# First attention: row maxima through VectorE's transpose and transfers, and a visit for two groups of heads

## The chip, the cores and the metric

The kernel runs on one core of one Trainium2 chip. The metric is device time in microseconds (us) of one execution, the median of several runs. A core has TensorE (matrix products; it writes only to PSUM, eight banks here), VectorE, ScalarE, GpSimd (POOL in the profile) and SyncE (SP), which here only issues transfers. Each engine works through its own instructions in the order of the program and waits on semaphores.

## The reference, cut to what matters

Input `x` is 16 batches of 256 tokens of 128 channels. Four layers follow, each added to `x`: an attention with binarised weights (the one that is changed), a mixture of eight experts, a second attention with relative positions, the experts again. The first attention:

```python
def _binarize(W):
    alpha = jnp.mean(jnp.abs(W), axis=tuple(range(1, W.ndim)), keepdims=True)
    B = W + jax.lax.stop_gradient(jnp.sign(W) - W)
    return alpha * B
...
B, T, C = x.shape                      # 16, 256, 128
H = HEADS                              # 16
Dh = C // H                            # 8
scale = Dh ** (-0.5)
q = split_heads(_binlinear(x, Wq, bq))
k = split_heads(_binlinear(x, Wk, bk))
v = split_heads(_binlinear(x, Wv, bv))
att = jnp.einsum('bhtd,bhsd->bhts', q, k) * scale
att = jax.nn.softmax(att, axis=-1)
y = jnp.einsum('bhts,bhsd->bhtd', att, v)
y = y.transpose(0, 2, 1, 3).reshape(B, T, C)
return _binlinear(y, Wp, bp)
```

Its `x` is layer-normalised first. The experts need the gate's logits of all tokens, so the first attention's last steps for a batch also normalise the result, turn it to channels and compute the logits.

## The kernel before

**Groups.** A batch has 16 heads, handled as four groups (`NG`) of four heads (`NJ`). G counts groups over all batches, 0 to 63; batch b has groups 4b to 4b+3. The queries and keys of a batch lie in one tile `spread[b % 4]` (`a_qk` in the profile): head j of a group sits on partitions 32j to 32j+31, of which row 32j is a spare row and the next eight hold the head's eight channels. In the spare row the queries have 0 and the keys 1 (`aux`).

**Steps of a group.**

- `scores(G, j)` computes head j's 256 x 256 scores into one PSUM bank with two matmuls that use only the 32 rows of that head, so matmuls of different j can run beside one another. VectorE then reduces the bank to minus the row maximum (L458, `a_nm<-a_s`, a tile of two columns per head).
- `maxima(G)` turns those maxima with two full TensorE transposes against the identity (L467) and VectorE adds them to the queries (L473): the sum, `qaug` (`a_qa`), has minus the maximum of each query in its spare row.
- `exponentials(G, j)` multiplies keys by `qaug` (L481, `a_t`), so the scores arrive transposed and with the maximum taken off, since the spare row of the keys is 1. ScalarE takes the exponential (L487, `a_pT<-a_t`).
- `values(G)` handles two groups at once with 32 matmul passes of 32 columns each (L497); ScalarE copies the result (L506).

**Steps of a batch.** `channels` (transpose the normalised tokens, L406), `project` (queries and keys; ScalarE adds the bias, SP stores the result to DRAM at L423 and loads it back spread over the rows at L427, four loads), `project_v` (L436), `tokens` (transposes back and division by the sums, L514 to L524), `turn_back` (L532), `project_out` (L545, VectorE adds to `x`), `gate_channels` (L558) and `gate` (L566, logits).

**Order.** All engines follow the order in which the program was written. `together` runs generators in turns: first the TensorE part of each, then what reads it. The main loop runs over i, from 3 to 72. For each i it does two halves, each with `scores(i, ...)` of two heads and `exponentials(i-3, ...)` of the two *other* heads, and then `visit(i)`, which does the steps of batches that are due by `table` together with `maxima(i-1)` and, every second time, `values(i-4)`. So groups and visits alternate, and the exponentials follow the scores three groups later. `begin` sets up the first groups; in the last visits pieces of the following experts (`filling`) are put between.

**Banks.** `bank8` hands out the eight PSUM banks in a ring, and the loop reorders the ring after each group. A bank is written again only when its last reader is done.

**Weights.** `load_later` loads the second attention's weights and w1 after visit 5 and w2 after visit 9, each of w1 and w2 (2,048 KB) in one transfer.

Of the kernel before, what the change touches and what calls it, by code (L numbers as in the profile page):

```python
# [10 lines left out]
F32 = mybir.dt.float32  # L11
# [7 lines left out]
P = 128  # L19
# [27 lines left out]
def _consts():  # L47

    p = np.arange(P)
    parts = {  # L50
        "ident": np.eye(P),

        "aux": np.repeat(p[:, None] % 32 == 0, NG, axis=1),

        "mask_h": p[:, None] % DH == np.arange(DH)[None, :],
        "mask_q": p[:, None] // DH % DH == np.arange(DH)[None, :],

        "digits": np.tile(
            np.concatenate([np.arange(1.0, NCAND + 1) * (1 << z) for z in SHIFTS]), (P, 1)
        ),  # L60
    }
    at = 0
    for name, a in parts.items():
        CONSTS[name] = (at, at + a.shape[1])
        at += a.shape[1]
    return np.concatenate([a.astype(np.float32) for a in parts.values()], axis=1)
# [12 lines left out]
def hybrid_kernel(ctx: ExitStack, tc: tile.TileContext, io):  # L79
# [31 lines left out]

    def load_later(step):

        for name, t in ((("b_w", b_w), ("w1", w1)), (("w2", w2),))[step]:
            nc.sync.dma_start(t, io[name])
        if step:
            nc.vector.tensor_copy(flips, const("digits"))
# [80 lines left out]
    def attention_a(place, filling):  # L198
# [4 lines left out]
        with ExitStack() as st:  # L203
# [5 lines left out]
            ring = deque(range(8))  # L209

            def bank8(name):
                i = ring.popleft()
                ring.append(i)
                return psum.tile([P, 2, T], F32, tag=f"x{i}", name=name, bufs=1)
# [5 lines left out]
            def spread_tile(fill):  # L220
                i = len(spread)
                t = wpool.tile([P, 2, NG, T], F32, tag=f"qk{i}", name=f"a_qk{i}")
                if fill:
                    nc.gpsimd.memset(t[:, 0], 0.0)
                    nc.gpsimd.tensor_copy(
                        t[:, 1], const("aux").unsqueeze(2).to_broadcast([P, NG, T])
                    )
                spread.append(t)
# [23 lines left out]
            def fills():  # L252

                wS["w"] = pool.tile([P, T], F32, tag="sw", name="wS_w", bufs=1)
                nc.gpsimd.memset(wS["w"], 0.0)
                for n in "qk":
                    wS[n] = pool.tile([P, NG, NJ, 32], F32, tag="sgn", name=f"wS_{n}")
                    nc.gpsimd.memset(wS[n], 0.0)
                for i in range(4):
                    nm = wpool.tile([P, 2, NJ, 32], F32, tag=f"nm{i}", name=f"a_nm{i}")  # L260
                    nc.gpsimd.memset(nm, 0.0)
                    nms.append(nm)
                values_tile()
# [33 lines left out]
            def begin():  # L297
# [30 lines left out]
                for i, n in enumerate("qk"):  # L328
                    nc.vector.tensor_scalar(
                        wS[n][:, :, :, 1 : 1 + DH],  # L330
                        pt[:, i].rearrange("p (g j d) -> p g j d", g=NG, j=NJ),
                        SCALE if n == "q" else 1.0, None, ALU.mult,
                    )
# [29 lines left out]
                for i in range(2):  # L363
                    spread_tile(True)
                    values_tile()
                    if not i:
                        nc.gpsimd.memset(ones, 1.0)
                        together(*(scores(0, j) for j in range(NJ)))
                        second = matmuls(1)
# [3 lines left out]
                        together(maxima(0, bank8("a_mx0")[:, 0]))  # L373
                        together(project(1))
                        together(*second)

                ring.rotate(4)
                third = matmuls(2)
                turns = maxima(1, bank8("a_mx1")[:, 0])
                next(turns)  # L380
                next(third[0], None)
                next(turns, None)
                pt = bank8("a_mv2")
                together(project_v(0, pt[:, 0]), channels(2, pt[:, 1]))
                together(*third[1:])
                used = list(ring)
                ring.clear()
                ring.extend(used[:2] + used[6:] + used[2:6])
                xns[3] = normalise(3)
                spread_tile(True)  # L390

            def matmuls(G):

                parts = [scores(G, j) for j in range(NJ)]
                for _ in range(2):
                    for g in parts:
                        next(g)
                return parts

            q, k, va, xnT, qaug, probs, heads, ys, yTs = ({} for _ in range(9))  # L400
# [10 lines left out]
            def project(b):  # L411

                pp = bank8(f"a_pqk{b}")
# [11 lines left out]
                for j in range(NJ):  # L425
                    at = 32 * j + 1
# [3 lines left out]
                    )  # L430
                q[b], k[b] = to[:, 0], to[:, 1]
# [15 lines left out]
            def scores(G, j):  # L447
# [4 lines left out]
                for t in range(2):  # L452
                    nc.tensor.matmul(  # L453
                        sc[:, t, :], q[b][rows, g, t * P : (t + 1) * P], k[b][rows, g, :],
                        start=True, stop=True,
                    )
                    yield
                nc.vector.tensor_reduce(  # L458
                    nms[G % 4][:, :, j, 0:1].rearrange("p t o -> p (t o)"),
                    sc, AX.X, ALU.max, negate=True,  # L460
                )

            def maxima(G, pm):

                b, g = divmod(G, NG)
                for t in range(2):
                    nc.tensor.transpose(  # L467
                        pm[:, t * P : (t + 1) * P],
                        nms[G % 4][:, t].rearrange("p j e -> p (j e)"), ident,
                    )  # L470
                yield
                qaug[G] = work.tile([P, T], F32, tag="qa", name=f"a_qa{G}")
                nc.vector.tensor_tensor(qaug[G], q[b][:, g, :], pm, ALU.add)  # L473

            def exponentials(G, j):
# [4 lines left out]
                for t in range(2):  # L480
                    nc.tensor.matmul(  # L481
                        sc[:, t, :], k[b][rows, g, t * P : (t + 1) * P], qaug[G][rows, :],
# [25 lines left out]
            def tokens(b):  # L508

                ys[b] = work.tile([P, 2, C], F32, tag="y", name=f"a_y{b}")  # L510
                po = bank8(f"a_oq{b}").rearrange("p t (c x) -> p t c x", x=P)
# [50 lines left out]
            def gate(b, pl):  # L562
                pl = pl[:, 0 : 2 * NE].rearrange("p (t e) -> p t e", e=NE)
                for t in range(2):
                    at = b % 2 * T + t * P
                    nc.tensor.matmul(  # L566
                        pl[:, t, :], xn2[b // 2][:, at : at + P], gw, start=True, stop=True
                    )
# [10 lines left out]
            def of(b):  # L579
# [3 lines left out]
            n, own = NB * NG, []  # L583
# [10 lines left out]

            table = (
                ([], [(gate, -3)], [(turn_back, -2)]),
                ([(project, 2)], [(project_out, -2)], []),
                ([], [], [(channels, 3)]),
                ([(tokens, -1)], [], [(project_v, 2), (gate_channels, -2)]),
            )  # L600

            extra = {3: ([(project, 2)], [], [(project_v, 1)]), 4: ([], [], [(channels, 3)])}

            def visit(i):
                b, s = divmod(i, NG)
                alone, with_maxima, with_values = (
                    [(f, b + d) for f, d in pieces if of(b + d)] + more
                    for pieces, more in zip(table[s], extra.get(i, ([], [], [])))
                )
                parts = []  # L610
                if i < n + 1 or with_maxima:
                    pt = bank8(f"a_mx{i}")
                    if i < n + 1:
                        parts.append(maxima(i - 1, pt[:, 0]))
                    parts += [f(b, pt[:, 1]) for f, b in with_maxima]
                parts += [f(b) for f, b in alone]
                pair = s % 2 == 0 and i < n + 4
                if pair or with_values:
                    pt = bank8(f"a_mv{i}")
                    parts += [f(b, pt[:, k]) for k, (f, b) in enumerate(with_values)]  # L620
                    if pair:
                        parts.append(values(i - 4, pt[:, 1]))
# [3 lines left out]
            own_at = {2: 2, 3: 3, 4: 3, 5: 3, 6: 3, 7: 4, 8: 2}  # L626
            for i in range(3, NG * (NB + 2) + 1):
                b, s = divmod(i, NG)
                for half in range(2 if i < n else 0):
                    together(  # L630
                        *(scores(i, 2 * half + j) for j in range(2)),
                        *(exponentials(i - 3, 2 - 2 * half + j) for j in range(2)),
                    )
                if n <= i < n + 3:
                    together(*(exponentials(i - 3, j) for j in range(NJ)))
                if i < n:


                    used = list(ring)
                    ring.clear()  # L640
                    ring.extend(used[k] for k in (2, 0, 3, 1, 6, 4, 7, 5))
                if i >= n + 2:
# [3 lines left out]
                    for _ in range(own_at.get(i - n, 0)):  # L646
                        own.append(next(filling))
                visit(i)
                if i in (5, 9):
                    load_later(i // 9)  # L650
                if i == 4 or s == 2 and of(b + 4):

                    xns[b + 3 + (s == 2)] = normalise(b + 3 + (s == 2))
# [900 lines left out]
def _spread(v, extra):  # L1554

    out = np.zeros((NJ, 32, NG), np.float32)
    out[:, 0] = extra
    out[:, 1 : 1 + DH] = v.reshape(NG, NJ, DH).transpose(1, 2, 0)
# [72 lines left out]
```

## Time and profile before

| | us |
|---|---|
| median of 3 runs | 1523.93 (1523.55 to 1524.88) |
| the profiled execution | 1522.07 |
| its span, first to last instruction | 1520.0 |
| scores of the first attention, first to last start | 13.7 to 275.6 |
| exponentials' matmuls, first to last start | 21.9 to 284.0 |
| last logits of the first attention | 313.9 |

In rows of groups, the profile gives line, engine, operation, output<-input by the program's names and the count; then busy time in us and the mean of one in ns; then the idle time of the engine before them and what ended it. In timelines: start and length in us, engine, line, operation and count. In a row of a stretch: the stretch, then busy time of TensorE, its weight loads, VectorE, ScalarE and POOL, each with the number of instructions, then TensorE's granted clock (1.00 is full), the share of the transfer engines that was busy, and GB/s. An f32 matmul is recorded as two passes, a transpose as one. In waits: who waited for what, us in total, times, and the longest.

Sizes of the parts in question over the whole run:

| line | what | count | mean ns |
|---|---|---|---|
| L453, TensorE | scores, passes | 1024 | 389 |
| L481, TensorE | exponentials' matmuls, passes | 1024 | 392 |
| L467, TensorE | transposes of the maxima | 128 | 301 |
| L458, VectorE | row maxima | 256 | 682 |
| L473, VectorE | maxima added to the queries | 64 | 408 |
| L487, ScalarE | exponentials | 256 | 602 |
| L427, SP | loads of queries and keys | 60 | 297 to issue |

The mean of a pass includes filling and draining the array; passes that follow one another overlap.

### The profile page before, as it was taken

The numbers are of one execution on the slowest core, as the hardware profiler recorded it, in microseconds if no ns is written. First come the engines' busy times: TensorE is split into PE (matmuls) and PEld (weight loads), VectorE is DVE, ScalarE is ACT, GpSimd is POOL, SyncE is SP. The second block draws the span as 40 slices with busy tenths as digits, with TensorE's granted clock in tenths as the row PEclk, the third lists the DMA queues.
The fourth block names the chain that finished last, engine by engine and source line by source line (L and its number), as shares of the span: only waits on it lengthen the run. The fifth ranks groups of instructions, "written<-read, shape, count | busy, mean of one in ns | idle before, by whom it ended". The sixth has DMA issues, their size and how long they took to land. (4 is left out here: it accounts for less than half of the span.)

```text
span 1520.0 us, 35594 instructions
## 1 busy us (share of the span) xinstructions
PE 1500.0 (99%) x14318; PEld 878.5 (58%) x14318; DVE 1119.3 (74%) x2055; ACT 853.2 (56%) x2119; POOL 416.6 (27%) x521
## 2 busy tenths in 40 slices
PE   8999999999999999999899999999999999999998
PEld 6777777544444444445577777777544444455554
DVE  7887877335467788899799999999345458878843
ACT  4666666644434444444688888888644444444442
POOL 6333331100001000041388888897100000000000
PEclk9999999999999999999999999999999999999999
DMA  4511110000331202212122222222000440121220
GB/s 105 152 32 30 37 36 16 1 8 1 95 105 42 51 15 65 51 35 51 31 58 55 51 46 53 57 52 45 9 0 0 124 108 24 51 61 33 65 64 14
DMA packets 176732, 73.33 MB, mean 48 GB/s; under 512 B 75056, under 2 KB 175032, under 8 KB 176312
## 3 DMA queue, kind: packets, MB, share of 16 engines
q1 hardware_dynamic: 175928, 70.64, 19.7%
q8 instruction: 113, 1.85, 0.5%
q10 hardware_dynamic: 640, 0.42, 0.2%
q14 instruction: 51, 0.42, 0.1%
HBM read 51.04 MB, written 12.58 MB: 42 GB/s over the span
## 5 line engine op out<-in xcount | busy, mean ns | idle before, releaser
L1326 ACT ACTIVATE hT<-ph,head 128x512 f32<-128x512 f32 x320 | 220.1, 688 | 266.6 <-PE ph L1322 251.8
L1322 PE MATMUL ph<-xn,w 128*64 128x512 f32 (+1 forms) x1216 | 292.0, 593 | 0.5 <-ACT b_xnT L723 0.5
L901 ACT ACTIVATE b_pr<-b_s,b_nm 128x256 f32<-128x256 f32 x512 | 235.9, 473 | 62.4 <-DVE b_nm L896 62.0
L1340 DVE TENSOR_TENSOR hT<-hT,gb 128x1024 f32<-128x1024 f32 x144 | 178.4, 1239 | 38.3 <-ACT hT L1326 37.9
L1117 PE MATMUL py<-hT,w 128*128 128x512 f32 (+1 forms) x456 | 205.5, 594 | 1.0 <-ACT logits L987 0.5
L458 DVE TENSOR_REDUCE a_nm<-a_s 128x2 f32<-128x512 f32 x256 | 158.6, 682 | 50.5 <-PE a_t L481 49.3
L1322 PEld LDWEIGHTS ph<-xn,w 128*64 128x64 f32 (+1 forms) x1216 | 100.7, 140 | 146.5 <-issue 117.0
L1106 PE MATMUL ph<-xn,w 128*128 128x512 f32 x384 | 174.1, 594 | 2.4 <-ACT hT L1108 2.3
L1108 ACT ACTIVATE hT<-ph,head 128x512 f32<-128x512 f32 x192 | 131.0, 687 | 76.5 <-PE ph L1106 74.0
L896 DVE TENSOR_REDUCE b_nm<-b_s 128x4 f32<-128x1024 f32 x128 | 152.8, 1194 | 19.9 <-PE b_s L886 19.7
L886 PE MATMUL b_s<-b_kT,b_qd 64*64 64x256 f32 x1024 | 159.9, 382 | 3.5 <-ACT b_pr L901 3.5
L1377 PE MATMUL s_m<-mx,mix 128*64 128x256 f32 x576 | 158.6, 379 | 0.5 <-DVE mx L1346 0.5
L911 DVE STREAM_TRANSPOSE b_pT<-b_pr 128x1024 f32<-128x1024 f32 x128 | 157.2, 1228 | 0.0
L886 PE MATMUL b_s<-strip,b_qb 64*64 64x256 f32 x2048 | 156.6, 376 | 0.0
L886 PE MATMUL b_s<-b_kS,b_qd 64*64 64x256 f32 x1024 | 156.5, 382 | 0.0
L487 ACT ACTIVATE a_pT<-a_t 128x512 f32<-128x512 f32 x256 | 132.6, 602 | 29.6 <-PE a_t L481 29.3
L1377 PE MATMUL s_y<-hT,w 128*64 128x256 f32 x576 | 148.1, 379 | 0.0
L156 POOL TENSOR_SCALAR ve<-mv 128x2 f32<-128x2 f32 x64 | 16.3, 255 | 458.8 <-DVE mv L153 448.8
L1117 PEld LDWEIGHTS py<-hT,w 128*128 128x128 f32 x456 | 84.7, 191 | 94.6 <-issue 91.1
L481 PE MATMUL a_t<-a_qa,a_qk 32*128 32x256 f32 x1024 | 133.8, 392 | 0.1
L453 PE MATMUL a_s<-a_qk 32*128 32x256 f32 x1024 | 128.8, 389 | 0.3 <-ACT a_qkc L419 0.3
L1106 PEld LDWEIGHTS ph<-xn,w 128*128 128x128 f32 x384 | 72.0, 190 | 92.5 <-issue 83.8
(211 smaller groups left out, 2653.1 us busy)
## 6 DMA issues: line engine op xcount, KB each, us to landing
gb<-gd SPq DMA_DIRECT2D x128, 256.0 KB
w<-in_w SPq DMA_DIRECT2D x2, 2048.0 KB
a_qks<-a_qkc SPq DMA_DIRECT2D x15, 256.0 KB
a_qk<-a_qks SPq DMA_DIRECT2D x60, 64.0 KB
so<-sum SPq DMA_DIRECT2D x18, 128.0 KB
x<-in_x SPq DMA_DIRECT2D x16, 128.0 KB
b_qs<-b_qT SPq DMA_DIRECT2D x64, 32.0 KB
b_qsel<-b_qT SPq DMA_DIRECT2D x64, 32.0 KB
```

Source lines behind the costliest of these rows:

```text
L458: nc.vector.tensor_reduce(nms[G % 4][:, :, j, 0:1].rearrange("p t o -> p (t o)"), sc, AX.X, ALU.max, negate=True,)
L481: nc.tensor.matmul(sc[:, t, :], k[b][rows, g, t * P : (t + 1) * P], qaug[G][rows, :], start=True, stop=True,)
L886: nc.tensor.matmul(sc[64 * c : 64 * c + 64, r, u, :], (qb_[rows, at, c] if rel else qd[rows, at, x]).rearrange("p h q -> p (h q)"), strip[ ...
L896: nc.vector.tensor_reduce(nm, sc, AX.X, ALU.max, negate=True)
L901: nc.scalar.activation(pr[:, u, r, :], sc[:, r, u, :], AF.Exp, bias=nm[:, r, u : u + 1], scale=1.0, accum_out=sums[b][:, n : n + 1],)
L911: nc.vector.transpose(pT[:, half % 2, 4 * i : 4 * i + 4].rearrange("p n k h q -> p (n k h q)"), probs.pop(U).rearrange("p u r k -> p (u r ...
L1106: nc.tensor.matmul(ph, w1[:, m * P : (m + 1) * P], xn2[c], start=True, stop=True)
L1117: nc.tensor.matmul(py[:, 0:width], w2[:, e * NHC + k, :], hs[k], start=k == 0, stop=k == NHC - 1)
L1322: nc.tensor.matmul(ph[z], w1[:, m * P + z.start : m * P + z.stop], xn2[c], start=True, stop=True,)
L1326: nc.scalar.activation(h[:, k % 2], ph, AF.Gelu_apprx_tanh, bias=b1[:, m : m + 1], scale=1.0)
L1340: nc.vector.tensor_tensor(h, h, gb.unsqueeze(1).to_broadcast([P, 2, CH]), ALU.mult)
L1377: nc.tensor.matmul(acc[halves[z], col], a[:, k], b[:, k], start=e == 0 and region[i] not in region[:i], stop=e == NE - 1 and region[i] not ...
```

## The change

- **The spare row** moves from row 32j to row 32j+8, behind the eight channels. The keys' half of the tile is filled with 1 everywhere before the channels are loaded, so its spare row is 1; `aux` goes.
- **Row maxima.** `maxima` and `qaug` go. After the last head's reduction of a group, VectorE transposes the maxima in blocks of 32 x 32 (`turned`), and four transfers on SP, one per head, write them straight into the spare row of the queries. For that, the scores use every second token as stationary operand (`t::2`), so that a block holds 64 neighbouring tokens. `exponentials` reads the queries themselves.
- **Reset.** The scores need 0 in the spare row. From the fifth batch on, `project` adds a transfer that copies a row of zeros into it.
- **Order.** The loop runs over n; for each n the groups 2n and 2n+1 follow one another, each as two halves: `scores` of heads 0 and 1, then `exponentials` of heads 0 and 1 of the group four earlier, then the same with heads 2 and 3. After the two groups comes one `visit(n)` with the steps of two former visits, full-array steps ahead of those that use 32 columns, and `values` in every visit.
- **Gate.** The gate's two matmuls per batch become eight that use 32 columns each.
- **Banks** are handed out least recently used first.
- **Weights** are loaded in 17 transfers of 256 KB, one per visit from n = 3 on.

```diff
+    pieces = [(b_w, io["b_w"])]
+    for t, name in ((w1, "w1"), (w2, "w2")):
...
+        pieces += [(t[:, at : at + CH], flat[:, at : at + CH]) for at in range(0, NE * HID, CH)]
...
-            ring = deque(range(8))
-
-            def bank8(name):
-                i = ring.popleft()
-                ring.append(i)
+            used = [*range(8)]
+
+            def bank8(name, among=range(8)):
+                i = next(i for i in used if i in among)
+                used.remove(i)
+                used.append(i)
                 return psum.tile([P, 2, T], F32, tag=f"x{i}", name=name, bufs=1)
...
-                    nc.gpsimd.tensor_copy(
-                        t[:, 1], const("aux").unsqueeze(2).to_broadcast([P, NG, T])
-                    )
+                    nc.gpsimd.memset(t[:, 1], 1.0)
...
                 for j in range(NJ):
-                    at = 32 * j + 1
+                    at = 32 * j
...
+                if b >= 4:
+                    nc.sync.dma_start(to[DH::32, 0], to[DH + 1 :: 32, 0])
...
                     nc.tensor.matmul(
-                        sc[:, t, :], q[b][rows, g, t * P : (t + 1) * P], k[b][rows, g, :],
-                        start=True, stop=True,
+                        sc[:, t, :], q[b][rows, g, t::2], k[b][rows, g, :], start=True, stop=True
                     )
                     yield
+                nm = nms[G % 4]
                 nc.vector.tensor_reduce(
-                    nms[G % 4][:, :, j, 0:1].rearrange("p t o -> p (t o)"),
-                    sc, AX.X, ALU.max, negate=True,
-                )
-
-            def maxima(G, pm):
...
+                    nm[:, :, j], sc, AX.X, ALU.max, negate=True
+                )
+                if j < NJ - 1:
+                    return
+                turned = work.tile([P, 32, 2], F32, tag="nmT", name=f"a_nmT{G}", bufs=4)
+                nc.vector.transpose(turned.rearrange("p x t -> p t x"), nm)
+                for n in range(NJ):
+                    row = spread[b % 4][32 * n + DH : 32 * n + DH + 1, 0, g, :]
+                    nc.sync.dma_start(row, turned[n::32])
...
-                        sc[:, t, :], k[b][rows, g, t * P : (t + 1) * P], qaug[G][rows, :],
+                        sc[:, t, :], k[b][rows, g, t * P : (t + 1) * P], q[b][rows, g, :],
...
                 for t in range(2):
-                    at = b % 2 * T + t * P
-                    nc.tensor.matmul(
-                        pl[:, t, :], xn2[b // 2][:, at : at + P], gw, start=True, stop=True
-                    )
+                    for y in range(4):
+                        at = b % 2 * T + t * P + 32 * y
+                        nc.tensor.matmul(
+                            pl[32 * y : 32 * y + 32, t, :], xn2[b // 2][:, at : at + 32], gw,
+                            start=True, stop=True,
+                        )
...
+            shared = (
+                (
+                    [(tokens, -2)],
+                    [(channels, 2), (project_out, -3)],
+                    [(gate, -4)],
+                ),
+                (
+                    [(project, 2)],
+                    [(turn_back, -2), (gate_channels, -3)],
+                    [(project_v, 1)],
+                ),
+            )
...
+                    if valued:
+                        parts.append(values(pair, pt[:, 1]))
                 together(*parts)
...
-            for i in range(3, NG * (NB + 2) + 1):
-                b, s = divmod(i, NG)
-                for half in range(2 if i < n else 0):
-                    together(
-                        *(scores(i, 2 * half + j) for j in range(2)),
-                        *(exponentials(i - 3, 2 - 2 * half + j) for j in range(2)),
-                    )
...
+            own_at = {33: 2, 34: 3, 35: 3, 36: 3, 37: 4, 38: 5}
+            for n in range(1, 2 * NB + 7):
+                for i in (2 * n, 2 * n + 1):
+                    for half in range(2):
+                        if i < NG * NB:
+                            together(*(scores(i, 2 * half + j) for j in range(2)))
+                        if 0 <= i - 4 < NG * NB:
+                            together(*(exponentials(i - 4, 2 * half + j) for j in range(2)))
...
+                visit(n)
+                load_later(n - 3)
```

## The prediction, as put on record before the changed kernel was seen

> **What bounds the kernel now.** I read the page first, then the busy times of one steady stretch, then TensorE's own timeline, and last the two engines that empty its banks.
>
> ```profile
> PE 1500.0 (99%) x14318; PEld 878.5 (58%) x14318; DVE 1119.3 (74%) x2055; ACT 853.2 (56%) x2119; POOL 416.6 (27%) x521
> ...
> 151.03:167.86 16.83, 16.82 (x230) 12.36 (x227) 13.54 (x33) 11.14 (x25) 5.77 (x9) 1.00 0.15 34
> ```
>
> The second line is one batch of the first attention (four groups): 16.83 us, TensorE busy throughout at full clock (1.00), VectorE 13.54 of it, ScalarE 11.14. The three batches from 117.36 on all take 16.83 or 16.84. So TensorE's order sets the pace, and its timeline is the view to cost from:
>
> ```profile
> 151.03 0.44 PE L467 MATMUL a_mx<-head,a_nm 128*128 128x128 f32 x2
> 151.30 0.61 PE L545 MATMUL a_mx<-wp,a_yT 128*128 128x128 f32 x4
> 151.75 0.60 PE L415 MATMUL a_pqk<-a_xnT,wq 128*128 128x256 f32 x2
> 152.18 0.59 PE L415 MATMUL a_pqk<-a_xnT,wk 128*128 128x256 f32 x2
> 152.71 0.48 PE L453 MATMUL a_s<-a_qk 32*128 32x256 f32 x2
> 152.72 0.48 PE L481 MATMUL a_t<-a_qa,a_qk 32*128 32x256 f32 x2
> 153.03 0.38 PE L453 MATMUL a_s<-a_qk 32*128 32x256 f32 x2
> ...
> 153.47 0.58 PE L481 MATMUL a_t<-a_qa,a_qk 32*128 32x256 f32 x3
> 153.69 0.38 PE L453 MATMUL a_s<-a_qk 32*128 32x256 f32 x2
> ...
> 154.76 0.44 PE L467 MATMUL a_mx<-head,a_nm 128*128 128x128 f32 x2
> 155.04 0.38 PE L406 MATMUL a_mv<-head,xn 128*128 128x128 f32 x2
> 155.35 1.94 PE L497 MATMUL a_mv<-a_pT,a_va 128*32 128x256 f32 x32
> 157.22 0.48 PE L453 MATMUL a_s<-a_qk 32*128 32x256 f32 x2
> ```
>
> A record here is one pass; an f32 matmul of 256 columns has two. I subtract starts, since lengths overlap. Between 153.03 and 153.69 a step takes 0.22 us and holds four passes, two a_s and two a_t, one on each group of 32 rows. A group of heads is eight steps, 1.73 us; entering the 32-row shape costs 0.10 more (152.71 to 153.03 is 0.32) and leaving it 0.09. So 1.92 is the floor; the four groups of this batch take 2.05, 1.94, 2.17 and 1.98, together 8.15. The other 8.68 is visits: full-array passes of 0.112 (four in 151.30 to 151.75), or 0.215 with 256 columns, 0.15 for changing over, and 1.87 for values (155.35 to 157.22).
>
> **The change part by part.**
>
> *Removed from TensorE:* two transposes a group, 0.27 us (151.03 to 151.30), 1.1 a batch, and two of four visits, each with its 0.15. The VectorE addition behind them goes too (64 of 408 ns); VectorE is not the bound over a batch, so I cost that at nothing.
>
> *The new visits,* by those units. Even: 10 full passes (tokens 4, channels 2, project_out 4) 1.12 + 0.15, the gate as 16 narrow passes four abreast, values 1.87. The gate's nearest row is the weight load of a 32-column tile:
>
> ```profile
> L497 PEld LDWEIGHTS a_mv<-a_pT,a_va 128*32 128x32 f32 x1024 | 30.7, 109 | 22.0 <-issue 4.9 <-ACT a_pT L487 0.8 <-DVE a_nm L458 0.3
> ```
>
> Four steps of 0.11 are 0.44; 0.4 (the same passes now) to 0.9 (steps of 0.22) bound it. Even sum 3.58. Odd: project 4 x 0.215 = 0.86, eight passes 0.90, 0.15, values 1.87: 3.78. Together 7.36, against 8.68: 1.32 saved a batch.
>
> *The two groups without a visit between.* Undisturbed they would take 16 x 0.216 + 0.19 = 3.64. But a group uses eight banks, all there are: s0 s1 e0 e1 s2 s3 e2 e3 (s scores, e exponentials, the digit the row group). Banks are taken least recently first, so each tile of the second group waits until the same tile of the first is read. And where scores of rows 0, 1 were paired with exponentials of rows 2, 3, now both lie on the same rows, so no exponential finishes before four matmuls of its row group. The readers:
>
> ```profile
> 153.95 2.07 ACT L487 ACTIVATE a_pT<-a_t 128x512 f32<-128x512 f32 x4 [0.30 <-PE a_t L481]
> ...
> 154.00 2.45 DVE L458 TENSOR_REDUCE a_nm<-a_s 128x2 f32<-128x512 f32 x4
> ```
>
> Four exponentials take 2.07 and one about 0.60: they start 0.49 apart. Four reductions take 2.45 and one 0.68: 0.59 apart. ScalarE starts 0.25 after the last pass has streamed (pass from 153.48, plus 0.22, to 153.95). In-order waits are seen here:
>
> ```profile
> 22.66 0.18 PEld L481 LDWEIGHTS a_t<-a_qa,a_qk 32*128 32x128 f32 x1 [0.50 <-ACT a_xnT L409]
> 22.67 0.19 PEld L453 LDWEIGHTS a_s<-a_qk 32*128 32x128 f32 x2
> ```
>
> The a_t load waits for ScalarE, whose copy ends 22.61 (0.05 to come back); the a_s loads of other row groups, free since 22.4, start only behind it. Now from the start of a stretch: s0 to s3 are full at 0.10 + 4 x 0.216 = 0.97, e0 to e3 at 1.83. Reductions start at 1.22 and end at 1.90, 2.49, 3.08, 3.67; exponentials start at 2.08 and end at 2.68, 3.17, 3.66, 4.15. The second group, with 0.05 back and 0.10 for a load not made ahead: s0 from 1.95, s1 from 2.54, e0 behind s0 from 2.91, e1 from 3.51. s2 stands in program order behind e1's wait (3.22) and runs to 4.18; s3 waits for the fourth reduction, 3.72, and runs 0.96 to 4.68; e3, its bank back at 4.20, follows to 5.54. Leaving 0.09: **5.63 for two groups**.
>
> From below: were e3 bound by its own bank alone, 4.20 + 0.86 + 0.09 = 5.15. From above: no row shows a row group with eight passes queued while another one starts, only a short lead (the third a_t of 153.47 starts at 153.68, ahead of the a_s at 153.69 that precedes it in the program). With no lead only neighbouring halves overlap, three steps of two passes (0.43) a half: 13 x 0.43 + 0.19 = 5.8. I take 5.65: the two mechanisms agree within 0.2.
>
> The Trainium skill, "TensorE: Matmul & The Clock Gate", Part 3, says matmuls are strictly first in, first out, across tiles too. The rows at 153.68 and 153.69 speak against it; by the page the stretch would be 5.8 and the total some 5 us above mine.
>
> *VectorE's transpose* of 128x64 has no row of its shape. The nearest, 128x1024 at 1,228 ns, gives 0.08 by size; the shortest VectorE copy (logits, 166 ns) is the likelier floor. I take 0.17, one a group, behind the fourth reduction, where the next wait is not VectorE's; 0 to 1.2 bounds it, and at 1.2 the second group's reductions end 1 us later, still ahead of the next stretch.
>
> *The transfers.* SP issues 256 more, and from the fifth batch on a reset per batch. An issue of such a load takes 297 ns:
>
> ```profile
> SPq L427 <- DMA a_qks<-a_qkc: 29.6, 15, 3.2
> ...
> 22.30 1.36 SPq L427 DMA_DIRECT2D a_qk<-a_qks  x4
> ```
>
> A group's four need 4 x 0.3 = 1.2. The worst they stand behind is project's turn on SP: 3.2 for its store to land, 1.36 for four loads, 0.3 for the reset, 0.43 for a weight piece, some 2 before it for ScalarE's turn: 7.3. With landing (3.2 again) 11.7. A row is turned about 3.8 into its stretch and read two stretches later, 15 us on: hidden, costing nothing. Were that cover gone, every wait for it would stand on TensorE. The reset is read three visits later, likewise hidden. Weights in 17 pieces replace three loads at visits that end long before their first use (after 284 us): nothing. POOL's fill is 0.95 instead of 1.06 us, three times, before the loop: nothing. Queries taken every second column as weights: loads are 185 ns under a 216 ns step; no row shows a stride, so 0 to a doubling (a score pass of 0.37), and I take 0.
>
> *Sum.* A batch: 2 x 5.65 + 7.36 = 18.66 against 16.83: +1.83. Sixty of 64 groups run scores and exponentials together: 15 batches, **+27.4**. At the edges one group's exponentials and one values (2.9) move behind the last scores, while first and last visits lack pieces in both kernels: -4 to +5, taken as 0. The profiled run took 1522.07 (span 1520.0), so 1549.5; the median shown, 1523.93, lies 1.86 above: **1551**.
>
> **The rivals.**
>
> *Banks come back in time.* Then a stretch is 3.64, a batch 14.64, 2.19 x 15 = 33 saved: 1491. For it: all the removed passes are real, and VectorE (13.5 less 1.6 of 14.64) and ScalarE (11.14) would fit on average. Against it: eight reductions at 0.59 need 4.7 us in a stretch of 3.64, and only eight banks hold them. The sign turns at a stretch of 4.74 (16.83 - 7.36, halved); the last exponential's bank alone gives 5.15. 9 in 100; a draw 2.
>
> *Strict order:* 5.8 a stretch, 15 x 2 x 0.15 more: 1556. For it, no deep lead is shown; against it, the short one is. 25 in 100.
>
> *Row transfers or dependencies reach TensorE.* If scores of a group waited for the previous group's rows in the same tile, 64 x about 3 us: 1740. Against: scores begin at 13.70 while ScalarE writes other groups' slices of that tile up to 14.65. A milder form, strided loads at the doubled price, adds 0.15 to eight steps per group at most: 64 x 1.2 = 77. 9 in 100 together.
>
> **How the numbers follow.** Forecast 55 in 100, the rivals 9, 2, 25, 9. Forecast and strict order reach from a stretch of 5.15 (30 x 0.5 = 15 less, and the edge's -4: 1532) to one of 5.8 with slow gates (15 x 0.46 = 7), waits of 0.3 a stretch that I do not see (9) and an edge of +3: 5 + 7 + 9 + 3, 1575. Faster means below 1520.9, slower above 1527.0: 0.2%, what a measurement of this kernel can tell. Faster 0.09, same 0.02, slower 0.89.
>
> **What would show it.** Right: from 60 us on, a stretch of a_s and a_t 5.5 to 5.8 long with gaps in which row groups stand, waits of a_s and a_t for a_nm and a_pT; visits of 3.6 and 3.8; no TensorE wait for a transfer. Wrong: stretches under 4.7, or TensorE waiting for a_qk transfers, or score passes more than 0.22 apart where nothing waits.

## The result and the profile after

| | median, us | runs | profiled execution | its span |
|---|---|---|---|---|
| before | 1523.88 | 1523.55 to 1524.88 (4) | 1522.07 | 1520.0 |
| after | 1546.49 | 1545.48 to 1548.74 (4) | 1545.72 | 1543.6 |

The changed kernel is slower: 1.0149 times the kernel before, interval 1.0132 to 1.0167, or 22.6 us. Forecast were 1551 within 1532 to 1575.

The lines of after that answer to the first two shown of before are the page's busy times and one batch in the view of windows. In the second the columns are length, busy time and number of instructions for PE, PEld, DVE, ACT and POOL, granted clock, DMA share and GB/s:

```profile
PE 1521.8 (99%) x14382; PEld 913.4 (59%) x14382; DVE 1113.8 (72%) x2055; ACT 855.1 (55%) x2119; POOL 416.3 (27%) x521
...
125.69:144.01 18.32, 18.32 (x234) 14.69 (x230) 13.25 (x32) 11.35 (x24) 5.76 (x10) 1.00 0.31 60
```

A batch has grown from 16.83 us to 18.32 or 18.33, in both batches I laid a window over. 15 batches at 1.49 or 1.50 more make 22.4, and the interval of the measured 22.6 us is 20.1 to 25.4, so the loss lies in the steady loop. The two traces agree: the last logits of the first attention come at 337.2 us instead of 313.9, 23.3 of the 23.6 us by which the spans differ. TensorE counts as busy throughout in both kernels at full clock. What changed is how much each microsecond does, and busy time doesn't show that; the timeline does. One stretch of two groups in after, TensorE (start, length, operation, passes):

```profile
125.69 1.14 PE L434 MATMUL a_s<-a_qk 32*128 32x256 f32 x8
126.66 0.38 PE L456 MATMUL a_t<-a_qk 32*128 32x256 f32 x2
126.67 0.49 PE L434 MATMUL a_s<-a_qk 32*128 32x256 f32 x2
126.88 0.38 PE L456 MATMUL a_t<-a_qk 32*128 32x256 f32 x2
...
128.20 0.49 PE L434 MATMUL a_s<-a_qk 32*128 32x256 f32 x2
...
129.40 0.48 PE L434 MATMUL a_s<-a_qk 32*128 32x256 f32 x1
...
130.16 1.24 PE L456 MATMUL a_t<-a_qk 32*128 32x256 f32 x8
131.32 0.48 PE L394 MATMUL a_m<-a_xnT,wq 128*128 128x256 f32 x1
```

and VectorE under it:

```profile
126.86 2.49 DVE L439 TENSOR_REDUCE a_nm<-a_s 128x2 f32<-128x512 f32 x4 [0.86 <-PE a_s L434]
129.38 0.25 DVE L445 STREAM_TRANSPOSE a_nmT<-a_nm 128x64 f32<-128x64 f32 x1
129.54 2.45 DVE L439 TENSOR_REDUCE a_nm<-a_s 128x2 f32<-128x512 f32 x4
```

From 125.69 to 131.32 is 5.64 us, against 3.64 for the same passes without a wait. For the first 0.97 us the eight passes are a_s alone, two row groups at work and two idle; then four row groups; then less and less. The four reductions of the first group run from 126.86 to 129.34, and the last tile of the second group's scores starts at 129.40, as the fourth bank comes back. When the next visit starts at 131.32, VectorE is at the last reduction of the second group (to 131.99). How much of the loss is VectorE's pace and how much the order on TensorE, the experiments part.

The whole batch, with the visits taken from the same timelines by subtracting starts:

| us | before | after, forecast | after, measured |
|---|---|---|---|
| four groups | 8.15 | 2 x 5.65 = 11.30 | 2 x 5.64 = 11.28 |
| even visit | | 3.58 | 3.24 |
| odd visit | | 3.78 | 3.81 |
| all visits | 8.68 | 7.36 | 7.05 |
| batch | 16.83 | 18.66 | 18.33 |

### The profile page after: what moved, and what is told of

Same layout as the page of the kernel before. It is cut to its first block, busy times and chain, and to the rows that moved or that the text cites. A ratio compares the mean times of both kernels' runs of the same rounds, so it can differ in the third digit from the quotient of the medians.

```text
span 1543.6 us, 36649 instructions
## 1 busy us (share of the span) xinstructions
PE 1521.8 (99%) x14382; PEld 913.4 (59%) x14382; DVE 1113.8 (72%) x2055; ACT 855.1 (55%) x2119; POOL 416.3 (27%) x521
## 5 line engine op out<-in xcount | busy, mean ns | idle before, releaser
L881 DVE STREAM_TRANSPOSE b_pT<-b_pr 128x1024 f32<-128x1024 f32 x128 | 157.2, 1228 | 0.0
L434 PE MATMUL a_s<-a_qk 32*128 32x256 f32 x1024 | 151.6, 410 | 0.0
L456 PE MATMUL a_t<-a_qk 32*128 32x256 f32 x1024 | 144.6, 375 | 0.0
```

The source lines that it names most:

```text
L434: nc.tensor.matmul(sc[:, t, :], q[b][rows, g, t::2], k[b][rows, g, :], start=True, stop=True)
L881: nc.vector.transpose(pT[:, half % 2, 4 * i : 4 * i + 4].rearrange("p n k h q -> p (n k h q)"), probs.pop(U).rearrange("p u r k -> p (u r ...
```

## The experiments

All times below are from runs beside the kernel before on the same chip (its median there is 1522.97 to 1523.57). "Stretch" and "group" are from the start of the first a_s pass to the start of the next visit.

**e1_rows: the same visits, the two halves of a group on different rows.** In after, scores and exponentials of one half lie on the same 32-row groups. Here they alternate on opposite ones, as before.

```diff
-                        if i < NG * NB:
-                            together(*(scores(i, 2 * half + j) for j in range(2)))
-                        if 0 <= i - 4 < NG * NB:
-                            together(*(exponentials(i - 4, 2 * half + j) for j in range(2)))
+                        together(
+                            *(scores(i, 2 * half + j) for j in range(2) if i < NG * NB),
+                            *(
+                                exponentials(i - 4, 2 - 2 * half + j)
+                                for j in range(2)
+                                if 0 <= i - 4 < NG * NB
+                            ),
+                        )
```

> Exponentials lie on the other two row groups again and are interleaved with the scores. Theory (same-row order delays the exponentials and the first group's reads of the banks): all four row groups run from the start, the second group's last tiles start behind the fourth reduction at 3.7 us and end one tile later, a stretch of 4.8 instead of 5.64: 30 x 0.85 = 25 us less, 1521. Rival (two groups without a visit are what costs, whatever the rows): 5.6 a stretch, 1546. Rival (strided weights, transfers): no change, 1546.

Measured: 1527.27 us, ratio 1.0029 (1.0019 to 1.004). The stretch is 4.97, the batch 2 x 4.97 + 7.05 = 16.99. Its TensorE timeline:

```profile
194.65 0.49 PE L434 MATMUL a_s<-a_qk 32*128 32x256 f32 x2
194.66 0.48 PE L456 MATMUL a_t<-a_qk 32*128 32x256 f32 x2
...
196.28 1.37 PE L434 MATMUL a_s<-a_qk 32*128 32x256 f32 x4
197.27 0.57 PE L456 MATMUL a_t<-a_qk 32*128 32x256 f32 x2
...
199.62 0.44 PE L489 MATMUL a_m<-head,a_oT 128*128 128x128 f32 x2
```

All four row groups work from the first step on (the first four passes, two a_s and two a_t, start within 0.02 us), and the first eight steps pass without a wait. The second group still has to wait for banks: between 196.28 and 197.27 four passes start, where there was room for some eighteen (0.99 by 0.216, four abreast). VectorE, which reads the first group's scores one tile after another, returns them at that pace:

```profile
195.82 2.49 DVE L439 TENSOR_REDUCE a_nm<-a_s 128x2 f32<-128x512 f32 x4 [2.78 <-PE a_t L456]
```

The first two of these reductions end at 196.51 and 197.11; the second group's first passes for the same two tiles start at 196.57 and 197.16. So the order within the halves accounts for 1.34 of the 1.50 us a batch, and the banks keep the stretch 1.3 above 3.64. The stretch had been expected at 4.8: 30 times 0.17 is 5 of the 6 us by which the time lies above 1521.

**e2_split: a visit after each group, order of the halves as in after.** The first two entries of each visit, all full-array steps, go between the two groups; the third (gate or `project_v`, and `values`) stays behind the second. `visit(n, between)` runs the entries of its list with `at < 2` on the first call and the rest on the second:

```diff
+                    if i == 2 * n:
+                        visit(n, True)
-                visit(n)
+                visit(n, False)
```

> The full-array half of each visit is put between the two groups; the order of scores and exponentials stays that of the change. Theory (a row group takes only one matmul beyond the one that runs, so the halves follow 0.99 us apart whatever the banks do): a group takes 1.83 + 0.99 + 0.09 = 2.9 by itself, two take 5.8 and one more change of shape 0.25: some 9 us slower than the changed kernel, 1555. Rival (the missing visit between the groups is the cause): groups of 1.94 as before the change, 30 x 1.5 = 45 less, 1501.

Measured: 1571.43 us, ratio 1.0307 (1.0273 to 1.0342). The missing visit alone is not the cause: without its neighbour a group takes 2.92. One group of it:

```profile
208.63 1.14 PE L434 MATMUL a_s<-a_qk 32*128 32x256 f32 x8
209.60 0.38 PE L456 MATMUL a_t<-a_qk 32*128 32x256 f32 x2
209.62 0.49 PE L434 MATMUL a_s<-a_qk 32*128 32x256 f32 x2
210.59 1.03 PE L456 MATMUL a_t<-a_qk 32*128 32x256 f32 x8
211.55 0.31 PE L542 MATMUL a_m<-head,xn 128*32 128x8 f32 x16
```

Three half-width steps of about 0.98 each, where the floor for the same passes is 1.92 in all: the order alone costs 1.0 a group even where no bank is awaited. The visits grow as well: 19.22 a batch less 4 x 2.92 is 7.54, 0.49 more than in after, close to the two more changes of shape at 0.25 that were expected. The total came out 16 us above the forecast. A steady batch takes 0.89 more than in after, 15 times that is 13 us where some 9 had been forecast (the forecast's own terms make 12). The rest lies outside the steady batches: by the start of group 12 this trace is 7.7 us behind after (69.6 against 61.9), only 1.8 of it steady. I did not follow it further.

**e3_rows_split: both edits at once.**

> Both edits together: other rows, and half a visit between the groups. Theory: the first group takes 1.94; the second starts behind a visit of 1.4 and waits at its last two tiles for the visit's two banks, which VectorE empties behind the fourth reduction (5.05 us): 2.1 to 2.7. With the visits and one more change of shape 7.9 to 8.5 us for two groups, against 9.17 for the changed kernel and 8.42 before it: 1508 to 1526. Rival (missing visit alone): as e2_split, 1501. Rival (transfers): 1546.

Measured: 1528.83 us, ratio 1.0043 (1.0027 to 1.0059); a batch 16.61. First groups take 1.94, the floor, but second groups 2.94 and 2.34. This is not the order any more; it is VectorE. Behind the first group that starts at 195.94 a visit follows, and at 199.33 the second group; the visit's banks are emptied only behind the first group's four reductions and the transpose (VectorE's timeline, and a pass of the second group on TensorE):

```profile
197.11 2.49 DVE L439 TENSOR_REDUCE a_nm<-a_s 128x2 f32<-128x512 f32 x4 [1.50 <-PE a_t L456]
199.63 0.25 DVE L445 STREAM_TRANSPOSE a_nmT<-a_nm 128x64 f32<-128x64 f32 x1
...
200.49 0.41 DVE L525 TENSOR_TENSOR x<-x,a_m 128x256 f32<-128x256 f32 x1
...
200.96 0.48 PE L456 MATMUL a_t<-a_qk 32*128 32x256 f32 x1
```

The last read of a visit's bank ends at 200.90, 5.0 after the first group began, and the tile that waits for it starts at 200.96. The visit behind the second group starts at 202.27, as VectorE ends one more reduction (202.21) and returns that visit's bank. Two groups with their visits take 16.61 / 2 = 8.30, inside the 7.9 to 8.5 that was expected; one kind of second group and the time lie outside their ranges. The steady gain of 0.22 a batch (3 us) is more than lost at the edges: the last logits of the first attention come at 320.1 us, 6 later than before. Why the edges lose that much was not followed.

**h_max: the readers cheaper, the order as in after.** `sc[:, :, 0:P]` instead of `sc` in the row maximum.

> The row maximum is taken over the first 128 of 256 keys (any number near the maximum serves the softmax, so what is computed stays the same up to rounding); a reduction shrinks from 0.59 to about 0.32 us. Theory (the fourth reduction hands back the bank that the last score tile needs): that bank is no longer last, the exponentials' banks are; a stretch of 5.2, 30 x 0.45 = 13 less, 1533. Rival (TensorE's own order sets the stretch, with banks free in time): 5.64 stays, 1546. Rival (VectorE's sum of work): 30 x 8 x 0.27 = 65 less.

Measured: 1539.26 us, ratio 1.0105 (1.0083 to 1.0128), stretch 5.28, from the first score pass to the next visit:

```profile
195.48 1.14 PE L434 MATMUL a_s<-a_qk 32*128 32x256 f32 x8
...
200.75 0.48 PE L394 MATMUL a_m<-a_xnT,wq 128*128 128x256 f32 x1
```

The stretch is shorter, so the reductions are a part of the cause; it is nowhere near what VectorE's sum of work would give, so they are not all of it. The time is 6 us above the forecast. 30 times 0.36 is 11 us less than after, and the difference of the two ratios gives 6, with an interval of some 4 to either side. In the trace the third stretch starts 3.1 us later than in after (38.5 against 35.4); why was not followed.

**h_both: exponentials cheaper as well**, `activation(pT[:, 0], sc[:, 0], AF.Exp)`, so that no bank comes back late.

> As h_max, and the exponentials are taken of the first 128 of 256 queries' columns per bank alone (values reads that half twice, so what comes out is not the attention): both readers are about twice as fast, the order on TensorE is that of the changed kernel. Theory (a row group holds one matmul beyond the running one, so halves follow 0.99 us apart even with banks free in time): 3 x 0.99 + 1.83 + 0.09 = 4.9 a stretch, 30 x 0.75 = 22 less than the changed kernel, 1524. Rival (strict order of matmuls): 13 steps, 5.8, no gain or slower, 1546 to 1551. Rival (rows fully apart, banks alone decide): 3.6 to 3.9, 30 x 1.8 = 54 less, 1492.

Measured: 1523.25 us, ratio 1.0007 (0.9994 to 1.002), stretch 4.90. What is left is order alone:

```profile
183.59 1.14 PE L434 MATMUL a_s<-a_qk 32*128 32x256 f32 x8
184.56 0.38 PE L456 MATMUL a_t<-a_qk 32*128 32x256 f32 x2
184.58 0.49 PE L434 MATMUL a_s<-a_qk 32*128 32x256 f32 x2
...
185.55 0.38 PE L456 MATMUL a_t<-a_qk 32*128 32x256 f32 x2
185.56 0.49 PE L434 MATMUL a_s<-a_qk 32*128 32x256 f32 x2
...
188.49 0.70 PE L394 MATMUL a_m<-a_xnT,wq 128*128 128x256 f32 x2
```

Scores of rows 2 and 3 start 0.99 us after those of rows 0 and 1, and 0.02 after the first exponential pass of rows 0 and 1, and so it repeats every 0.98. The exponentials' second matmuls, which stand ahead of these scores in the program, run later. A row group here takes in one matmul beyond the running one; a further one stops everything behind it. Neither strict order (5.8) nor free row groups (3.6 to 3.9) gives 4.90.

The three runs cut the loss of a stretch, 5.64 less 3.64 = 2.0, into what slow maxima cost (0.36), what slow exponentials cost on top (0.38) and order (1.26). That split holds for this order of removal; the parts aren't independent, since e1 takes away the order and keeps 1.3 of banks.

**f1_alternate: the new path of the maxima with the old order around it.** Four visits a batch, opposite rows, exponentials three groups behind, banks given out as before, and the query and key loads issued one visit later:

```diff
+            for i in range(3, NG * (NB + 2) + 1):
...
+                    together(
+                        *(scores(i, 2 * half + j) for j in range(2)),
+                        *(exponentials(i - 3, 2 - 2 * half + j) for j in range(2)),
+                    )
...
+                while loads:
+                    loads.pop(0)()
+                if i < n:
+                    used[:] = [used[k] for k in (2, 0, 3, 1, 6, 4, 7, 5)]
...
+                visit(i)
```

> The order of before the change (a visit after each group, exponentials three groups later on the other rows, banks in the order of before) with the new way of the maxima: VectorE's transpose and four transfers; the narrow gate and the split weight loads stay; the loads of a batch's queries and keys are issued one visit later. Theory (the way of the maxima is a gain, the order around it took it back): before the change a batch took 16.83; two transposes of the maxima less per group (4 x 0.27) and the gate 0.25 less, with some bank waits more as the visits are shorter: 15.5 to 15.9, 16 x 0.9 to 1.3 less than before, 1503 to 1509. Rival (the transfers cost what the transposes did, by landing late): 1523 or more, with waits of a_t for transfers.

Measured: 1515.6 us, ratio 0.9956 (0.9944 to 0.9968), a batch 16.11. The batch lies 0.2 above the upper end of what was expected, the time 7 above. Three groups take 1.94 to 2.00, the one behind the visit of tokens 2.70, 0.76 above the floor. VectorE around that visit (188.33 to 189.58), and TensorE where the group stands:

```profile
187.56 2.48 DVE L449 TENSOR_REDUCE a_nm<-a_s 128x2 f32<-128x512 f32 x4 [0.81 <-PE a_t L466]
190.08 0.24 DVE L455 STREAM_TRANSPOSE a_nmT<-a_nm 128x64 f32<-128x64 f32 x1
190.25 0.32 DVE L508 RECIPROCAL a_rs<-a_m_tokens 128x32 f32<-128x32 f32 x1
190.60 0.42 DVE L509 TENSOR_TENSOR a_y<-a_m_tokens,a_rs 128x256 f32<-128x256 f32 x1
...
190.56 0.60 PE L444 MATMUL a_s<-a_qk 32*128 32x256 f32 x4
191.13 0.57 PE L466 MATMUL a_t<-a_qk 32*128 32x256 f32 x2
```

The transpose, which nobody awaits soon, stands ahead of the division that gives the visit's bank back; the division ends at 191.03, and the exponentials' passes go on at 191.13.

**f2_alternate_lru: f1 without the line that permutes `used`**, so that banks go strictly by last use.

> As f1_alternate, but banks are taken least recently used first, without the order of before. Theory (banks decide between stretches): the visit's banks are those of the scores, which VectorE frees last, so waits grow by 0.2 to 0.5 a group: 64 x 0.35 = 22 more than f1_alternate, some 1528. Rival (banks do not matter): as f1_alternate within 3.

Measured: 1517.19 us, ratio 0.9959 (0.9945 to 0.9972), a batch 16.23. The larger loss I expected from it did not come; in this order of work the banks' sequence is worth 0.12 a batch.

**f3_late_turn: f1 with transpose and row transfers issued after the visit, and the bank of the visit of tokens given out last.**

```diff
+                def turn():
+                    turned = work.tile([P, 32, 2], F32, tag="nmT", name=f"a_nmT{G}", bufs=4)
...
+                    turns.append(turn)
+                ahead = bank8(f"a_mv{i}") if s == 3 and with_values else None
...
                 visit(i)
+                while turns:
+                    turns.pop(0)()
```

> f1_alternate with two moves: VectorE's transpose of the maxima and its transfers are issued after the visit's own work, and the visit with tokens gives its bank out last, so that the next group meets it at its last exponential tile. Theory (the group after tokens takes 2.70 because its tiles wait for the bank that VectorE empties behind the fourth reduction and the transpose): 2.70 falls to 2.1 to 2.3, 15 x 0.5 = 7 less than f1_alternate, some 1508. Rival (rows that leave 0.3 to 1 us later are read three groups later and land late): waits of a_t for transfers, 1515 or more.

Measured: 1509.48 us, ratio 0.991 (0.9889 to 0.9931), some 14 us faster than before and 37 below the time of after. A batch takes 15.70; the group behind tokens 2.30:

```profile
183.80 2.49 DVE L449 TENSOR_REDUCE a_nm<-a_s 128x2 f32<-128x512 f32 x4 [0.38 <-PE a_t L473]
186.20 0.35 DVE L515 RECIPROCAL a_rs<-a_m_tokens 128x32 f32<-128x32 f32 x1
186.58 0.42 DVE L516 TENSOR_TENSOR a_y<-a_m_tokens,a_rs 128x256 f32<-128x256 f32 x1
186.92 0.23 DVE L457 STREAM_TRANSPOSE a_nmT<-a_nm 128x64 f32<-128x64 f32 x1
```

Division now follows the reductions and the transpose comes last. Which of the two moves brought the 0.40 was not tried. The two traces allow an estimate: in f1 the bank is back 1.45 after the group begins (191.03 less 189.58), in f3 1.19 (187.01 less 185.81), so some 0.26 would come from the transpose's place and the rest from the bank's.

The batches side by side:

| us | groups | visits | batch |
|---|---|---|---|
| before | 8.15 | 8.68 | 16.83 |
| after | 11.28 | 7.05 | 18.33 |
| e1 (opposite rows) | 9.94 | 7.05 | 16.99 |
| e2 (split visits) | 11.68 | 7.54 | 19.22 |
| e3 (both) | 9.16 | 7.45 | 16.61 |
| f1 (order of before) | 8.62 | 7.49 | 16.11 |
| f3 (late transpose) | 8.22 | 7.48 | 15.70 |

With four visits, the new path of the maxima and the narrow gate together take 1.2 us a batch out of them (by their rows before, 1.1 and 0.2: two transposes a group at 0.27, and a gate of 0.37 instead of 0.15); joining visits in pairs takes out another 0.4 and, with the order that came with it, costs 3.1 in the groups.

## Why the prediction was right, step by step

**What bounds.** Right: TensorE's order sets the pace in both kernels, and what moved the time is what moved on TensorE. VectorE is busy less than before in a batch (13.25 against 13.54) and matters only through when it gives a bank back.

**The two groups without a visit between.** Right in size and in mechanism: 5.65 forecast, 5.64 measured. The chain that was worked out stands in the trace, counted from the stretch's start at 125.69: fourth reduction over at 3.66 (forecast 3.67), last scores from 3.71 (3.72), next visit at 5.64 (5.63). h_max shows that the reductions are a part of it, e1 and h_both that the order is.

One step inside was wrong. I let scores of all four row groups start together; those of rows 2 and 3 start 0.99 later, as the timeline of after (126.67) and h_both show. That it did no harm was luck of this case: the readers take their tiles one after another, and the reductions still start 1.17, 1.78, 2.38 and 2.97 into the stretch (forecast 1.22, 1.81, 2.40, 2.99). In h_both, where readers are quick, the same error would have given 3.6 to 3.9 instead of 4.90.

**The visits.** Right in direction, and the gate mis-sized. A batch saves 1.63 in visits, forecast 1.32. I priced the 16 narrow gate passes by the weight load of a 32-column tile, four steps of 0.11; they take 123.84 less 123.69, 0.147 before rounding. 15 x (0.44 - 0.147) is 4.4 us, nearly the whole distance between the sum of 27.4 and the measured 22.6. The sign "visits of 3.6" did not show: the even visit takes 3.24. The steady timeline of after around the gate:

```profile
123.69 0.31 PE L542 MATMUL a_m<-head,xn 128*32 128x8 f32 x16
123.84 1.91 PE L472 MATMUL a_m<-a_pT,a_va 128*32 128x256 f32 x32
```

The recorded 110 ns of one weight load overlap those of the others here, since four abreast take 37 ns; the next step's start shows the price, and no row of before had eight-column passes in this shape.

**Costed at nothing.** The transpose, the stride and the transfers. Groups of instructions between 60 and 290 us (busy total, mean ns of one, idle time before):

```profile
L456 PEld LDWEIGHTS a_t<-a_qk 32*128 32x128 f32 x800 | 89.6, 185 | 6.8
L434 PEld LDWEIGHTS a_s<-a_qk 32*128 32x128 f32 x808 | 84.0, 191 | 13.1 <-issue 10.7
...
L445 DVE STREAM_TRANSPOSE a_nmT<-a_nm 128x64 f32<-128x64 f32 x50 | 12.3, 247 | 1.7
```

The transpose is recorded with 0.25, but VectorE's next instruction starts 0.17 after it (from 129.38), which is the 0.17 taken, though that came from a copy. In after nobody waits for it in time to matter, since the next scores wait for the fourth reduction ahead of it; in f1, where the order is better, its place begins to count (the estimate of 0.26 above). Loads of queries with stride two take 191 ns where contiguous ones take 185, still under a step of 0.216. SP's queue waits 46.4 us in that window for transposed maxima and 21.5 for project's store. The table of waits has no wait of TensorE for a transfer, but it has none for a late bank either. What speaks against one is that the readers' chain above accounts for the stretch to 0.01, and that f1 and f3 keep the row transfers and the split weights and are faster than before. One term here was mis-sized without effect: I took 297 ns for the issue of a row transfer, the price of the larger loads. It takes 492 (shortest, median and longest of 256, in ns):

```profile
L448 SPq DMA_DIRECT2D a_qk<-a_nmT x256: 492/492/934, 18.0 to 297.7; - x128
```

A group's four take 2.0 us of SP instead of 1.2. The cover of two stretches hid that as well.

**The rivals.** Banks in time (1491) falls: in after the banks are late, and h_both shows that even with quick readers the stretch is 4.90, about where the sign turns with the measured visits, (16.83 - 7.05) / 2 = 4.89; its time equals the kernel before's within the interval. Strict order (1556) falls on 5.64 and more clearly on 4.90. The page that I weighed, the Trainium skill, "TensorE: Matmul & The Clock Gate", Part 3, says that matmuls start strictly in program order; in after, scores of rows 2 and 3 start at 126.67, ahead of the second exponential matmuls at 127.09 that precede them, so here order is kept within a row group, and between row groups a short lead is possible. Transfers reaching TensorE falls by the same sums.

**The edges,** taken as 0, can't be told from 0 within the interval, but that is a balance. In the traces after is 2.0 us behind before at the start of group 12 (61.9 against 59.9), 18.5 at that of group 56 (263.4 against 244.9) and 23.3 at the last logits. The eleven batches between make 1.50 each; the two ahead of them lose 1.0 less than that, the two behind them 1.8 more.

**What would have shown it.** I named waits of a_s and a_t for a_nm and a_pT. They aren't in the table of waits: for these loads it prints only an issue wait of 0.4 at most, once a stretch. A likely reason, not shown, is that some row group is always busy, so that TensorE as a whole never counts as idle. Their place is the timeline, where starts that should be 0.22 apart stand further apart and coincide with the end of a reduction.

## What to carry to other kernels

When work is joined to save changes of shape, count the buffers that it uses before the next break and how soon their readers return all of them: here a stretch has eight reductions at 0.59 us, 4.7 in all, where its passes need 3.64, and eight banks don't cover the difference. Put neighbouring streams on different row groups, and give an engine that returns buffers its returns first and everything that nobody awaits last (f3, where this was moved together with a bank). A change that loses may hold a part that wins: this one's path for the maxima with the narrow gate, put into the old order with the two moves of f3, is 0.9% faster than the kernel before.

## What the hardware showed that I had not expected

- As the traces read, a group of 32 rows queues a single matmul beyond the running one. With banks free in time (h_both), halves that alternate on the same rows start 0.98 to 0.99 us apart, neither at once nor in strict order.
- Sixteen passes with a weight tile of 128x32 and eight columns each, on four column groups, take 0.147 us, 37 ns for every four, though one weight load is recorded with 110 ns.
- VectorE's transpose of 128x64 f32 is recorded with 247 ns, three times what scaling 128x1024 (1,228 ns) down by size would give; the next instruction starts 168 ns after it.
- TensorE at 99% busy and full clock in after, with half of its row groups idle for a sixth of a stretch (the first 0.97 of 5.64 us): here the busy share says nothing of how full the array is.
